# Running sums in PSUM for the first layer's Strassen products, and the last layer's weight sums moved from GpSimd to VectorE

## The chip, the core and the metric

The kernel runs on one core of one Trainium2 chip. The time is device microseconds; the lower, the better. The engines are named as in the profile: PE (TensorE matmul) with PEld (its weight loads), DVE (VectorE), ACT (ScalarE), POOL (GpSimd) and SP (SyncE, which issues most of the DMAs).

## The reference

Two layers run one after the other on `x` of 32 sequences x 128 tokens x 512 channels, all in float32.

```python
# layer 0: attention with 16 heads of 64, then experts chosen by the tokens' gates
shift = silu(t) @ W_ada.T + b_ada
h = _ln(x, ln1_g, ln1_b) + shift
qkv = (h @ Wqkv.T).reshape(b, n, 3, H, HD)
q = _ln(qkv[:, :, 0]...); k = _ln(qkv[:, :, 1]...); v = ...       # q and k are normalized per head
o = softmax(q k^T / sqrt(HD)) v
x = x + o @ Wout.T
tok = x.reshape(-1, d)
gate = softmax(tok @ Wgate.T)
vals, idx = top_k(gate.T, bs // E)          # E = 8 experts, each takes its best 512 of 4096 tokens
y = gelu(_ln(tok[idx]) @ fc1s[e].T + b1s) @ fc2s[e].T + b2s
tok = tok.at[idx].add(y * vals)
# layer 1: attention with 16 heads of 32, then an MLP of 2048, both behind an adaptive layer norm
normed = _layernorm(x) * (1 + scale) + shift
x = x + softmax(q k^T / sqrt(HD)) v @ wo.T + bo
x = x + gelu(normed @ w1.T + b1) @ w2.T + b2
```

## The kernel before

**Products.** Nearly all matmuls are done by Strassen's scheme in Winograd's form: a product of 2 x 2 blocks takes seven block products instead of eight, at the price of sums of blocks on both sides. With A and B cut into blocks and S and T for the block sums, the seven products are numbered 1: A11 B11, 2: A12 B21, 3: S4 B22, 4: A22 T4, 5: S1 T1, 6: S2 T2, 7: S3 T3. The four results are 1+2, 1+6+5+3, 1+6+7+4 and 1+6+7+5. In the last layer the MLP does this on two levels, 7 x 7, and needs sums of weights for it.

**First layer** (`pair`, some 60 to 940 us of the span). Sixteen pairs of sequences. From pair 1 on, the projections to q and k (two column groups, `q0` and `q1`) and to v are three calls of `seven` for each pair. A product there is two matmuls of 128 x 512 in float32, four matmul instructions. In the kernel before, each of the seven products has a PSUM bank of its own (`ps`, seven names; a bank is held from its product until it has been read). ScalarE copies product 1 to SBUF (`U1`, L1513) and VectorE makes seven additions (`comb`, L1509), each with one operand in PSUM: the running sums U2, U3, U4 in SBUF, and the four results. For q and k, ScalarE squares each result (`square`, L1471) and VectorE sums the squares per head (L1473). `back` does the attention of a sequence: transposes, scores, exponentials, sums, outputs. `project` is the output projection of a pair, again seven products (L1756, four matmuls of 128 x 256 each), with the residual `xt` added half by half: `onto` adds a running sum in SBUF, `out2` (L1772) a product in PSUM. For the last eight pairs (`LATE` is 16 sequences) the attention output is parked in DRAM and projected after all pairs (`late_projection`), while VectorE searches for the gates' thresholds.

**Experts** (`expert`, some 1060 to 1920 us). Eight experts. POOL makes the sums of the experts' weights, VectorE the additions to PSUM (`comb`, L2109, and `comb2`) and the masks `oh` of the next expert's tokens (L1926, 128 x 1024 in bf16); other block sums (`hs`, `tg`) go to either.

**Last layer** (from some 1920 us on). Here each set of seven products already uses three PSUM banks X, Y and Z: products 6, 7 and 4 are accumulated on top of product 1 in X, product 3 on top of product 5 in Z, and X and Z are read between (`chain_T`, L2571; `chained`, L2882; `seeded`, L2800). The sums of its MLP weights are made ahead and put in DRAM: 22 steps (`w1_outer`, `w2_outer`, `w1_inner`, `w2_inner`), each with four fetches of 256 KB, four sums (`weight_forms`) and four or seven stores. In the kernel before, four steps stand beside each of experts 0 to 4 and two beside expert 5, and POOL makes the sums. The like sums for wq, wk, wv and wo stand beside pairs 10 to 13, on VectorE.

**Order.** Every operation is given to a scheduler (`Sched`) with its engine or engines (`also`), an estimated duration, the buffers that it reads and writes, a priority and a job (pairs are jobs 0 to 15, then one for the routing, the experts, the last layer). The scheduler plays the program through with these estimates, admits jobs in a window of three, and on each engine takes what can start soonest, then what has the lowest priority number. The order found is the order of the program; each engine then runs its own list in order and waits on semaphores. `tt` is the helper for sums of two blocks in SBUF: VectorE (L1277) or POOL (L1278). It marks its operation with `port`: from job `lock_at` on, the plan lets no such operation of VectorE start while one of POOL runs, and the reverse. `lock_at` is the last layer's first job here. `keep` is the number of banks that must stay free when an operation takes one, `spare` the same for SBUF rows.

Of the kernel before, what the change touches and what calls it, by code (L numbers as in the profile page):

```python
# [186 lines left out]
class Op:  # L187
    __slots__ = ("alts", "prio", "job", "keep", "deps", "n", "ready", "next", "bufs", "lat", "done", "table", "seq", "mb", "port")


class Sched:
# [12 lines left out]
    def op(self, eng, us, fn, w=(), r=(), prio=0.0, job=0, keep=0, spare=0, lat=0.0, table=None, also=(), share=1.0, port=False):  # L204
# [5 lines left out]
        o.port = port  # L210
# [40 lines left out]
    def run(self):  # L251
# [46 lines left out]
        while left:  # L298
# [54 lines left out]
            for x in o.next:  # L353
                x.n -= 1
                wait = 0.0 if (len(x.alts) == 1 and e in x.alts and not lat) else self.WAIT[e]
                x.ready = max(x.ready, end + lat + wait)
# [804 lines left out]
def fast_kernel(ctx: ExitStack, tc: tile.TileContext, x, condT, mask, cols, w_ada, wqkv, wout, wout_p, wout_o, wgate,  # L1161
# [259 lines left out]
    def weight_sums():  # L1421
# [7 lines left out]
        for n in range(2):  # L1429
            for i, a_, b_, r_ in ((1, lambda n=n: wB(1, 2, n), lambda n=n: wB(1, 1, n), [wqkv_b[n + 2], wqkv_b[n]]),  # L1430
# [3 lines left out]
                tt(lambda i=i, n=n: wT(i, n), a_, b_, ALU.subtract, 2 * D, [wTb(i, n)], r_, 155, 1, DVE, False)  # L1434

    def pair(g):
# [48 lines left out]
        else:  # L1485
# [11 lines left out]
            def seven(name, B, T, pr, done):  # L1497

                ps = {m: bank(f"{name}{m}_{g}") for m in range(1, 8)}
                U1, U2, U3, U4 = (row(f"{name}u{m}_{g}") for m in "1234")  # L1500

                def prod(m, lhs, lb, rhs):
                    def f_():
                        for k in range(2):
                            nc.tensor.matmul(ps[m].t, lhs()[:, k, :], rhs[0](k), start=(k == 0), stop=(k == 1))  # L1505
                    sch.op(PE, mm_us(D, 2), f_, w=[ps[m]], r=[*lb, *rhs[1]], prio=pr, job=job, keep=3)

                def comb(o_, a_, m):
                    sch.op(DVE, dve_us(D), lambda: nc.vector.tensor_tensor(flat(o_), a_.t, ps[m].t, ALU.add), w=[o_],  # L1509
                           r=[a_, ps[m]], prio=pr, job=job)  # L1510

                prod(1, lambda: A(1, 1), rA(1, 1), B(1, 1))
                sch.op(ACT, act_us(D), lambda: nc.scalar.copy(U1.t, ps[1].t), w=[U1], r=[ps[1]], prio=pr - 1, job=job)  # L1513
                prod(2, lambda: A(1, 2), rA(1, 2), B(2, 1))
                done(comb, 1, 1, U1, 2)
                prod(6, lambda: Sv(2), [Sb[2]], T(2))
                comb(U2, U1, 6)
                prod(7, lambda: Sv(3), [Sb[3]], T(3))
                comb(U3, U2, 7)
                prod(5, lambda: Sv(1), [Sb[1]], T(1))  # L1520
# [878 lines left out]
    for n, step in enumerate(steps):  # L2399
        e = n // 4  # L2400
        step(5000.0 + 1000 * e + 800, RJ + 1 + e)
# [658 lines left out]
```

## Time and profile before

| | |
|---|---|
| median of 3 runs | 3227.43 us (3227.32 to 3228.43) |
| the profiled execution's own time | 3228.02 us |
| its span in the profile | 3226.3 us |
| mean granted clock of PE | 0.99 |
| PE busy | 3122.8 us (97%) |
| DVE busy | 2389.7 us (74%) |
| ACT busy | 1171.3 us (36%) |
| POOL busy | 1124.2 us (35%) |
| DMA | 460.02 MB, mean 143 GB/s |

Busy time is the sum of the time in which an engine has an instruction under way[...]. A line such as `L1277` is the line of the kernel that issued the instruction; since helpers issue many of them, the names of the tiles tell which they are. A wait is put down to the operation that came last before the waiting one went on. Queries of the trace by stretches of time show which engine limits a stage; the totals above mix stages with different limits.

### The profile page before, as it was taken

The numbers are of one execution on the slowest core, as the hardware profiler recorded it, in microseconds if no ns is written. First come the engines' busy times: TensorE is split into PE (matmuls) and PEld (weight loads), VectorE is DVE, ScalarE is ACT, GpSimd is POOL, SyncE is SP. The second block draws the span as 40 slices with busy tenths as digits, with TensorE's granted clock in tenths as the row PEclk, the third lists the DMA queues.
The fourth block names the chain that finished last, engine by engine and source line by source line (L and its number), as shares of the span: only waits on it lengthen the run. The fifth ranks groups of instructions, "written<-read, shape, count | busy, mean of one in ns | idle before, by whom it ended". The sixth has DMA issues, their size and how long they took to land. (4 is left out here: it accounts for less than half of the span.)

```text
span 3226.3 us, 60396 instructions
## 1 busy us (share of the span) xinstructions
PE 3122.8 (97%) x22740; PEld 2539.3 (79%) x22740; DVE 2389.7 (74%) x4834; ACT 1171.3 (36%) x2962; POOL 1124.2 (35%) x858
## 2 busy tenths in 40 slices
PE   9999999999999999989899999999999999999988
PEld 5655665555568888778788888989899999898988
DVE  8877767888778886876776536776868686868685
ACT  4333333434430212221122214545454545353533
POOL 0111110000030477767766520333333333333335
PEclk9999999999999999999999999999999999999999
DMA  4111112232245564676445261655655565555557
GB/s 174 47 57 46 44 44 69 89 99 64 64 146 174 158 185 155 189 211 187 160 156 158 79 193 35 202 185 166 188 161 187 161 190 165 183 175 173 181 178 228
DMA packets 293455, 460.02 MB, mean 143 GB/s; under 512 B 29930, under 2 KB 111394, under 8 KB 293154
## 3 DMA queue, kind: packets, MB, share of 16 engines
q1 hardware_dynamic: 284498, 438.43, 42.7%
q0 software_dynamic: 7168, 16.91, 2.7%
q8 instruction: 183, 3.00, 0.4%
q14 instruction: 118, 0.97, 0.1%
q10 hardware_dynamic: 1488, 0.71, 0.1%
HBM read 383.44 MB, written 72.51 MB: 141 GB/s over the span
## 5 line engine op out<-in xcount | busy, mean ns | idle before, releaser
L1278 POOL TENSOR_TENSOR base<-base,base 128x512 f32<-128x512 f32 x330 | 437.5, 1337 | 854.4 <-DVE base L2851 278.1
L2882 PE MATMUL bank<-base,base 128*128 128x128 f32 x3080 | 369.0, 277 | 14.0 <-DVE base L2727 7.7
L2800 PE MATMUL bank<-base,base 128*128 128x128 f32 x3080 | 376.3, 277 | 6.0 <-DVE base L1277 3.1
L2800 PEld LDWEIGHTS bank<-base,base 128*128 128x128 f32 x3080 | 366.5, 193 | 12.6 <-ACT bank L2761 3.5
L2882 PEld LDWEIGHTS bank<-base,base 128*128 128x128 f32 x3080 | 355.0, 192 | 24.9 <-DVE base L2727 9.5
L1277 DVE TENSOR_TENSOR base<-base,base 128x512 f32<-128x512 f32 (+2 forms) x487 | 298.4, 636 | 18.7 <-PE bank L2882 3.6
L2115 ACT ACTIVATE h<-h,prm 128x256 f32<-128x256 f32 x256 | 115.2, 500 | 324.0 <-DVE h L2109 314.7
L2168 PE MATMUL d<-fc,h 128*128 128x256 f32 x992 | 221.8, 383 | 0.6 <-PE pi L1946 0.4
L2168 PEld LDWEIGHTS d<-fc,h 128*128 128x128 f32 x992 | 189.6, 192 | 27.4 <-ACT h L2115 0.6
L2104 PE MATMUL u<-gT,fc 128*128 128x256 f32 x768 | 182.8, 389 | 23.5 <-DVE h L2109 22.8
L2810 ACT ACTIVATE base<-base,prm 128x128 f32<-128x128 f32 x512 | 169.9, 395 | 48.1 <-DVE base L2845 28.3
L2104 PEld LDWEIGHTS u<-gT,fc 128*128 128x128 f32 x768 | 149.8, 196 | 46.5 <-DVE h L2109 24.0
L1471 ACT ACTIVATE sq<-qk 128x512 f32<-128x512 f32 x128 | 81.3, 635 | 283.0 <-DVE qk L1509 271.1
L2104 PE MATMUL u<-tg,s 128*128 128x256 f32 x512 | 124.9, 388 | 13.0 <-DVE h L2109 8.0
L2104 PEld LDWEIGHTS u<-tg,s 128*128 128x128 f32 x512 | 98.9, 194 | 29.0 <-issue 8.6
L2109 DVE TENSOR_TENSOR h<-v,u 128x512 f32<-128x512 f32 x128 | 86.2, 681 | 45.9 <-PE u L2104 44.6
L2845 DVE TENSOR_TENSOR base<-bank,base 128x512 f32<-128x512 f32 x96 | 66.0, 687 | 72.1 <-PE bank L2800 56.8
L2168 PE MATMUL d<-t,hs 128*128 128x256 f32 x512 | 113.4, 379 | 0.0
L1505 PE MATMUL q<-wqkv,hsb 128*128 128x512 f32 x240 | 113.4, 595 | 0.0
L1505 PE MATMUL q<-t,hsa 128*128 128x512 f32 x240 | 112.8, 592 | 0.0
L1505 PE MATMUL q<-wqkv,hT 128*128 128x512 f32 x240 | 111.5, 598 | 0.0
L2727 DVE TENSOR_TENSOR base<-bank,base 128x128 f32<-128x128 f32 x168 | 47.7, 288 | 82.5 <-PE bank L2882 67.7
(1154 smaller groups left out, 6703.7 us busy)
## 6 DMA issues: line engine op xcount, KB each, us to landing
base<-w1i SPq DMA_DIRECT2D x224, 256.0 KB, 3.3
base<-w2i SPq DMA_DIRECT2D x224, 256.0 KB, 3.5
base<-w2s SPq DMA_DIRECT2D x168, 256.0 KB, 3.0
fc<-in_fc_dram SPq DMA_DIRECT2D x64, 512.0 KB, 7.6
fc<-in_fc_dram SPq DMA_DIRECT2D x32, 1024.0 KB, 8.5
base<-w1s SPq DMA_DIRECT2D x96, 256.0 KB, 3.4
base<-in_w_dram SPq DMA_DIRECT2D x72, 256.0 KB, 3.7
x<-in_x_dram SPq DMA_DIRECT2D x32, 256.0 KB, 3.7
```

Of the source, the lines that this page charges most:

```text
L1277: ways = {DVE: (DVE, dve_us(n), lambda: nc.vector.tensor_tensor(o_(), a_(), b_(), op_)), POOL: (POOL, 0.2 + n / 480, lambda: nc.gpsimd.ten ...
L1278: POOL: (POOL, 0.2 + n / 480, lambda: nc.gpsimd.tensor_tensor(o_(), a_(), b_(), op_))}
L1471: sch.op(ACT, act_us(D), lambda: nc.scalar.activation(sq.t, qk[i][j].t, AF.Square), w=[sq], r=[qk[i][j]], prio=pr, job=job)
L1505: nc.tensor.matmul(ps[m].t, lhs()[:, k, :], rhs[0](k), start=(k == 0), stop=(k == 1))
L2104: nc.tensor.matmul(ps[n].t[:, t, :], lhs()[:, k, t * P : (t + 1) * P], rhs.t[:, k, :], start=(k == 0), stop=(k == 1))
L2109: sch.op(DVE, dve_us(D), lambda: nc.vector.tensor_tensor(o_.t, a_.t, ps[n].t, ALU.add), w=[o_], r=[a_, ps[n]], prio=pr, job=job)
L2115: sch.op(ACT, act_us(HQ, 1), lambda t=t, c=c: nc.scalar.activation(o_.t[:, t, :], o_.t[:, t, :], AF.Gelu_apprx_tanh, bias=col("b1s", e * 1 ...
L2168: nc.tensor.matmul(ps[n].t[:, j, :], lhs[m].t[:, k, t * P : (t + 1) * P], rhs.t[:, 2 * m + k, :], start=(m == 0 and k == 0), stop=(m == NM ...
L2800: nc.tensor.matmul(b_.t[:, u, :], w_.t[:, u * P : (u + 1) * P], x_(), start=fresh and u == 0, stop=True, skip_group_check=True)
L2810: sch.op(ACT, act_us(S, 1), lambda k=k, u=u, c=c: nc.scalar.activation(o_[k].t[:, u * S : (u + 1) * S], o_[k].t[:, u * S : (u + 1) * S], A ...
L2845: sch.op(DVE, dve_us(D), lambda: nc.vector.tensor_tensor(d_[k].t, flat(src), first[k].t, ALU.add), w=[d_[k]], r=[src, first[k]], prio=po - ...
L2882: nc.tensor.matmul(b_.t, x_()[:, k * S : (k + 1) * S], w_.t[:, k, :], start=fresh and k == 0, stop=True, skip_group_check=True)
```

## The change

In `seven` and in `project`, the seven products use three banks X, Y, Z, in the order 1 (X), 5 (Z), 2 (Y), 6 (onto X), 3 (onto Z), 7 (onto X), 4 (onto X); in `seven` products 3 and 7 stand in this order, and product 4 last. Between the accumulations X and Z are read. In `seven` the readings are four copies (`kept`: u1, t_, u2 and one result; ScalarE or VectorE, whichever the plan finds free) and three VectorE additions. In `project` they are seven additions to the residual by VectorE, and `onto` and the copy are gone.

The sums of `weight_forms` go from POOL to VectorE, and the 22 steps from experts 0 to 5 to pairs 3 to 13, two steps beside each pair. Their fetches no longer wait for an expert (`ups`). Their stores get `late`, by which the plan has their readers wait 8 us longer. The sums t12 and t4 of the q and k weights may run on POOL too. `lock_at` is 0: the plan takes the port into account from the start.

```diff
-    def op(self, eng, us, fn, w=(), r=(), prio=0.0, job=0, keep=0, spare=0, lat=0.0, table=None, also=(), share=1.0, port=False):
+    def op(self, eng, us, fn, w=(), r=(), prio=0.0, job=0, keep=0, spare=0, lat=0.0, table=None, also=(), share=1.0, port=False, late=0.0):
...
-                x.ready = max(x.ready, end + lat + wait)
+                x.ready = max(x.ready, end + lat + wait + x.late)
...
-                tt(lambda i=i, n=n: wT(i, n), a_, b_, ALU.subtract, 2 * D, [wTb(i, n)], r_, 155, 1, DVE, False)
+                tt(lambda i=i, n=n: wT(i, n), a_, b_, ALU.subtract, 2 * D, [wTb(i, n)], r_, 155, 1)
...
-            def seven(name, B, T, pr, done):
-                ps = {m: bank(f"{name}{m}_{g}") for m in range(1, 8)}
-                U1, U2, U3, U4 = (row(f"{name}u{m}_{g}") for m in "1234")
-                def prod(m, lhs, lb, rhs):
-                    def f_():
-                        for k in range(2):
-                            nc.tensor.matmul(ps[m].t, lhs()[:, k, :], rhs[0](k), start=(k == 0), stop=(k == 1))
-                    sch.op(PE, mm_us(D, 2), f_, w=[ps[m]], r=[*lb, *rhs[1]], prio=pr, job=job, keep=3)
-                prod(1, lambda: A(1, 1), rA(1, 1), B(1, 1))
-                sch.op(ACT, act_us(D), lambda: nc.scalar.copy(U1.t, ps[1].t), w=[U1], r=[ps[1]], prio=pr - 1, job=job)
-                prod(2, lambda: A(1, 2), rA(1, 2), B(2, 1))
-                done(comb, 1, 1, U1, 2)
-                prod(6, lambda: Sv(2), [Sb[2]], T(2))
-                comb(U2, U1, 6)
-                prod(7, lambda: Sv(3), [Sb[3]], T(3))
-                comb(U3, U2, 7)
-                prod(5, lambda: Sv(1), [Sb[1]], T(1))
-                done(comb, 2, 2, U3, 5)
-                comb(U4, U2, 5)
-                prod(4, lambda: A(2, 2), rA(2, 2), T(4))
-                done(comb, 2, 1, U3, 4)
-                prod(3, lambda: Sv(4), [Sb[4]], B(2, 2))
-                done(comb, 1, 2, U4, 3)
+            def seven(name, B, T, pr, dest, done):
+                X, Y, Z = (bank(f"{name}{c}_{g}") for c in "xyz")
+                u1, u2, t_ = (row(f"{name}{c}_{g}") for c in "rst")
+                def prod(b_, lhs, lb, rhs, fresh, also=(), keep=0):
+                    def f_():
+                        for k in range(2):
+                            nc.tensor.matmul(b_.t, lhs()[:, k, :], rhs[0](k), start=fresh and k == 0, stop=True, skip_group_check=True)
+                    sch.op(PE, mm_us(D, 2), f_, w=[b_], r=[*lb, *rhs[1], *also], prio=pr, job=job, keep=keep)
+                def comb(i, l, a_, b_):
+                    o_ = dest(i, l)
+                    sch.op(DVE, dve_us(D), lambda: nc.vector.tensor_tensor(flat(o_), a_.t, b_.t, ALU.add), w=[o_], r=[a_, b_], prio=pr, job=job)
+                    done(i, l)
+                def kept(o_, src):
+                    copy([o_], [src], lambda: flat(o_), lambda: src.t, D, pr - 60, job)
+                prod(X, lambda: A(1, 1), rA(1, 1), B(1, 1), True, [Y, Z], 2)
+                prod(Z, lambda: Sv(1), [Sb[1]], T(1), True)
+                kept(u1, X)
+                prod(Y, lambda: A(1, 2), rA(1, 2), B(2, 1), True)
+                kept(t_, Z)
+                prod(X, lambda: Sv(2), [Sb[2]], T(2), False)
+                comb(1, 1, Y, u1)
+                kept(u2, X)
+                prod(Z, lambda: Sv(4), [Sb[4]], B(2, 2), False)
+                prod(X, lambda: Sv(3), [Sb[3]], T(3), False)
+                comb(1, 2, Z, u2)
+                comb(2, 2, X, t_)
+                prod(X, lambda: A(2, 2), rA(2, 2), T(4), False)
+                kept(dest(2, 1), X)
+                done(2, 1)
...
+        X, Y, Z = (bank(f"w{c}_{g}", (P, HD)) for c in "xyz")
+        def out2(i, l, b_):
+            sch.op(DVE, dve_us(HD), lambda: nc.vector.tensor_tensor(half(i, l), b_.t, half(i, l), ALU.add),
+                   w=[(xt[i - 1], l)], r=[b_, (xt[i - 1], l)], prio=pr - 60, job=job)
+        prod(X, A(1, 1), *B(1, 1), True, [Y, Z], 1)
+        prod(Z, S_[1], *T(1), True)
+        out2(1, 1, X)
+        prod(Y, A(1, 2), *B(2, 1), True)
+        out2(2, 2, Z)
+        prod(X, S_[2], *T(2), False)
+        out2(1, 1, Y)
+        out2(1, 2, X)
+        prod(Z, S_[4], *B(2, 2), False)
+        prod(X, S_[3], *T(3), False)
+        out2(1, 2, Z)
+        send(1)
+        out2(2, 2, X)
+        prod(X, A(2, 2), *T(4), False)
+        out2(2, 1, X)
+        send(2)
...
-        sch.op(SP, 0.06, lambda: nc.sync.dma_start(b_.t, src), w=[b_], r=[*r, ups[job - RJ - 1]], lat=4.0, prio=pr, job=job, spare=12)
+        sch.op(SP, 0.06, lambda: nc.sync.dma_start(b_.t, src), w=[b_], r=r, lat=4.0, prio=pr, job=job, spare=12)
...
-        sch.op(SP, 0.06, lambda: nc.sync.dma_start(dst, flat(b_)), w=[(std, key)], r=[b_], lat=4.0, prio=pr, job=job)
+        sch.op(SP, 0.06, lambda: nc.sync.dma_start(dst, flat(b_)), w=[(std, key)], r=[b_], lat=4.0, prio=pr, job=job, late=8.0)
...
-            tt(lambda o_=o_: o_.t, lambda a_=a_: a_.t, lambda b_=b_: b_.t, op_, D, [o_], [a_, b_], pr, job, POOL, False)
+            tt(lambda o_=o_: o_.t, lambda a_=a_: a_.t, lambda b_=b_: b_.t, op_, D, [o_], [a_, b_], pr, job, DVE, False)
...
-        e = n // 4
-        step(5000.0 + 1000 * e + 800, RJ + 1 + e)
+        g = 3 + n // 2
+        step(200.0 * g + 190, g)
...
-    st.sch.lock_at = LJ
+    st.sch.lock_at = 0
```

## The prediction

> **What bounds the kernel now.** I read the busy time by stage first, cut at the kernel's own boundaries (200 to 900 us is first layer; each expert is one cut, experts 1 to 7 start at 1170, 1276, 1385, 1499, 1611, 1720, 1820; the last layer follows). Shown are the first layer, expert 3 and expert 6. Columns: length, busy us of PE, PEld, DVE, ACT, POOL, granted clock, DMA share, GB/s.
>
> ```profile
> 200.00:900.00 700.00, 699.91 (x4937) 410.57 (x4928) 535.72 (x1238) 271.34 (x706) 60.22 (x54) 1.00 0.21 65
> ...
> 1385.00:1499.00 114.00, 101.77 (x498) 89.14 (x497) 86.45 (x103) 23.15 (x52) 82.52 (x64) 0.94 0.58 173
> ...
> 1720.00:1820.00 100.00, 98.97 (x466) 86.78 (x465) 64.40 (x77) 22.44 (x50) 58.33 (x42) 1.00 0.37 98
> ```
>
> Two things are to be seen. In the first layer PE is never idle, so nothing there can be gained by relieving VectorE (77% busy) or ScalarE (39%); new waits there, however, add to the time one for one. And experts 1 to 5, the same work as expert 6, take 106, 109, 114, 112 and 109 us where expert 6 takes 100: 550 against 500, so 50 us are lost, part as PE idle and part as a lower clock. Expert 6 has no weight sums for the last layer; POOL is busy 58 us there, 76 to 84 in the others.
>
> Next the waits of PE, asked for 1400 to 1500, 1500 to 1600, 1600 to 1700 and 1700 to 1900 us (one answer line each), then PE, VectorE and POOL in order of time around the first of them:
>
> ```profile
> PE u L2104 <- DVE h L2109: 12.2, 1, 12.2
> PE u L2104 <- DVE h L2109: 10.0, 1, 10.0
> PE u L2104 <- DVE h L2109: 6.3, 1, 6.3
> PE u L2104 <- DVE h L2109: 1.0, 1, 1.0
> ```
>
> ```profile
> 1409.07 3.62 PE L2104 MATMUL u<-gT,fc 128*128 128x256 f32 x16
> 1433.56 5.91 PE L2104 MATMUL u<-gT,fc 128*128 128x256 f32 x16 [12.23 <-DVE h L2109]
> ```
>
> ```profile
> 1413.70 19.20 DVE L1926 TENSOR_TENSOR oh<-iota_jb,lo 128x1024 bf16<-128x1024 bf16 x1
> 1432.83 0.67 DVE L2109 TENSOR_TENSOR h<-v,u 128x512 f32<-128x512 f32 x1
> ```
>
> ```profile
> 1415.42 1.83 POOL L1278 TENSOR_TENSOR w1n_4f<-w1r,w1n_4f 128x512 f32<-128x512 f32 x1
> 1416.65 5.46 POOL L1278 TENSOR_TENSOR t<-fc,fc 128x512 f32<-128x512 f32 x4
> 1421.54 5.42 POOL L1278 TENSOR_TENSOR t<-fc,t 128x512 f32<-128x512 f32 x4
> 1426.42 5.39 POOL L1278 TENSOR_TENSOR fc<-fc,fc 128x512 f32<-128x512 f32 x4
> ```
>
> A VectorE operation with two SBUF inputs (`oh`, 1.22 us when free) stands for 19.20 us, until POOL's unbroken run of 15 sums ends at 1431.8. The PSUM addition queued behind it (L2109) then frees a bank for PE, which has idled 12.23 us and afterwards runs 16 matmuls in 5.91 us instead of 3.62: the half clock. The first three of the 15, from 1412.96 on, are sums for the last layer (`w1n_4f` and its like). Expert 6 shows the same thing without them:
>
> ```profile
> 1745.96 13.40 DVE L1277 TENSOR_TENSOR hs<-h,h 128x512 f32<-128x512 f32 x1 [0.97 <-ACT h L2115]
> ```
>
> ```profile
> 1760.83 1.97 PE L2104 MATMUL u<-tg,s 128*128 128x256 f32 x8 [1.03 <-DVE h L2109]
> ```
>
> A block of 13.40 us costs PE 1.03 us: PE's work ahead covers 12.4 us there, 7.0 at 1413 (19.20 less 12.23).
>
> **The change part by part.**
>
> *Weight sums to VectorE and to pairs 3 to 13 (two steps a pair).* The 22 steps have 4 sums each, 88 in all. They leave POOL, where sums in a run start 1.23 us apart: 108 us go, 16 sums or 20 us per expert in 0 to 4 and 8 sums in expert 5. On VectorE the nearest rows are the sums for wq, wk, wv and wo, which already run there in pairs 10 to 13:
>
> ```profile
> L1277 DVE TENSOR_TENSOR os__6712<-os__6701,oq 128x512 f32<-128x512 f32 x1 | 0.7, 694 | 0.0
> ```
>
> 88 x 0.69 = 61 us. Their DMAs move too: 88 fetches and 100 stores of 256 KB (4 and 4 a step, 7 stores in the four `w2_outer`), 48 MB. Pairs 3 to 13 take some 640 us (their first L1505 matmuls start at 195 and, for pair 14, at 838), so 75 GB/s join the 65 of the first row; 140 is less than the experts carry now. On SP's queue a store waits for its sum, and behind it wait loads of x, xT and the statistics; the sums of wq to wo with their stores already stand so in pairs 10 to 13, and PE has no wait there. I cost this at nothing; the cover is that loads land 3 to 4 us after issue and are early: from 200 to 900 us the normalization (L1600) waits 0.5 us in all for a transfer. If the cover fails, each late load stops PE for a few us.
>
> *What this gives in the experts.* [...] The trace says that a VectorE operation stands until a whole run of POOL operations is over (19.20 us for 15). [...] By the row the gain is the 50 us. The measurement decides. What remains is POOL's run of 12 (`t`, `t`, `fc`: 1416.65 to 1431.8, 15 us), a block of up to 15 us; against a cover of 7 to 12 PE would wait 3 to 8 us, against expert 6's example 1 us. Bounds of the gain: 15 us (8 us and the colder clock in most experts) to 51. I take expert 6's 1 us in each of five: 50 - 4 = 46 us.
>
> *Planner's lock from the start, `late` of 8 us for stores, t12 sums also on POOL.* Only the order changes. The lock makes the plan know that `hs` cannot pass a POOL run, but `oh` isn't marked, so it can still be caught. Worth -5 to +5 us; I take 0, as nothing in the trace tells the sign.
>
> *The sevens on running sums.* 45 of them (three in each of 15 pairs). PE's work stays: 7 products of 4 matmul instructions. In PE's order of time, groups of eight instructions of 256 columns start 1.73 us apart, so four of 512 take 1.73. VectorE's PSUM additions fall from 7 to 3, copies rise from 1 to 4:
>
> ```profile
> L1509 DVE TENSOR_TENSOR qk<-q0u,q 128x512 f32<-128x512 f32 x49 | 33.5, 683 | 25.7 <-PE q L1505 25.5
> L1513 ACT COPY q0u<-q 128x512 f32<-128x512 f32 x12 | 7.0, 587 | 17.7 <-PE q L1505 16.2 <-DVE xn L1600 1.5
> ```
>
> VectorE: -180 x 0.683 = -123 us, with the sums +61, so 62 us less over the 870 us of these pairs: 77% becomes about 70%. ScalarE: +135 x 0.587 = 79 us: 39% becomes 48%. Neither is the bound; this work lies beside PE. What lies on the path is new: before, each product had its own bank; now X is added to by products 6, 7 and 4 only after X was read. Between 1 and 6 stand two products, 3.5 us, for a copy of 0.59 us; between 6 and 7 one, 1.73 us; between 7 and 4 none of its own, so an addition of 0.68 us and two semaphores must be covered by another seven or by attention. Behind PE's waiting matmul everything of PE is queued. Three banks of eight are held for a whole seven.
>
> The trace of before has this scheme already, in the last layer:
>
> ```profile
>   DVE base L1277: 0.4, 1
>   issue: 0.2, 1
> ```
>
> ```profile
>   DVE base L2727: 17.2, 18
>   issue: 13.1, 30
> ```
>
> These are the idle lists of PE (us, times) by what ended the idle time: first of L2571, 32 chains of the last layer's projections, 0.6 us in all; then of L2882, 56 chains of its MLP, 36 us with the smaller entries. Per chain 0.02 to 0.64 us. Products there last half as long as here, so the cover was smaller. With 45 sevens and 16 projections, 61 chains: 1 to 39 us. I take 10, since L2571, two chains beside attention as here, is the nearer row.
>
> [...] If it came to the 0.94 of expert 3, 870 us would grow by 6%, 52 us, and the change would lose. But the last layer, made of such chains, has a granted clock of 1.00 here:
>
> ```profile
> 2400.00:2500.00 100.00, 96.81 (x968) 90.07 (x968) 82.14 (x179) 48.58 (x125) 35.19 (x27) 1.00 0.63 196
> ```
>
> So I add nothing for it.
>
> *Projections.* 16; PE's 7 products stay. From 3 + 4 PSUM additions, 4 SBUF additions and a copy to 7 PSUM additions of 0.42 us: 4 x 0.42 x 16 = 27 us less on VectorE and POOL, off the path. Their waits are in the 61 chains.
>
> *Sum.* The profiled execution took 3228.0 us (span 3226.3 and 1.7 around it), the median is 3227.4. 3228.0 - 46 + 10 = 3192.0; less 0.6 for the median, 3191 us.
>
> **The rivals.** (1) *POOL's own run of 12 is enough*: experts keep waits of 3 to 8 us, which cool the clock too, and half is recovered, 25 us: 3227 - 25 + 10 = 3212. For it: `oh` isn't marked. Against it: expert 6, which has the run and waits 1 us. (2) *The chains cost as L2882's do*, 36 to 39 us with the experts' 46: 3219. For it: VectorE at 70% and ScalarE at 48% now sit in PE's path. (3) *Slower: PE waits at X.* An addition or copy queued late behind ScalarE's squares (which waited 223.6 us for VectorE from 200 to 900) or VectorE's sums stops PE at products 7 and 4. It decides from 46 / 61 = 0.75 us per chain; at 1.0 us it is 61 us: 3242. Against it: 1.0 is above both rows. (4) *The planner's order is no better anywhere, or the moved sums hold up pairs*: gain and loss within a few us of each other, 3227.
>
> **How the numbers follow.** My forecast 0.55 (own range 3178 to 3203), rival 1 0.17, rival 2 0.13, rival 3 0.09, rival 4 0.06. Predicted 3191. The low end takes a full 51 us with chains at 1 us, 3177; the high end reaches into rivals 1 and 2, 3222. A measurement tells 0.2% (6.5 us) from no change. Faster 0.85, same 0.06, slower 0.09.
>
> **What would show it.** Right: experts 1 to 5 near 100 us each at clock 1.00, no VectorE operation above 15 us there, POOL near 58 us an expert; first-layer PE idle of some 10 us, put down to L1509's or a copy's successors. Wrong: blocks of 13 to 15 us with PE waits above 3 us (rival 1), PE waits for copies or additions in nearly every seven (rivals 2 and 3), PE waiting for transfers of x or xT between 300 and 850 us (SP's queue).

## The result, and the profile after

The changed kernel takes 3202.45 us (median of four runs, 3200.34 to 3203.46), beside 3227.93 for the kernel before in the same comparison: a ratio of 0.9917, 95% interval 0.9900 to 0.9934, so 25 us faster. Its profiled execution took 3203.46 us with a span of 3201.7.

Where did the 25 us come from? I cut both profiled spans at the same four points: the first L1505 matmul (pair 1's first product), the last L1505 matmul (the end of pair 15's products), the first matmul of expert 0 (L2104 before, L2090 after), and the first chained product of the last layer (L2571 before, L2557 after). Lengths in us:

| | before | after | difference |
|---|---|---|---|
| up to pair 1's first product | 66.7 | 87.4 | +20.7 |
| pairs 1 to 15, first to last L1505 matmul | 872.0 | 879.2 | +7.2 |
| late projections and hand-over to the experts | 129.7 | 130.2 | +0.5 |
| the eight experts | 863.3 | 810.1 | -53.2 |
| last layer | 1294.6 | 1294.8 | +0.2 |
| span | 3226.3 | 3201.7 | -24.6 |

So two large numbers stand against each other: the experts gave 53 us, more than forecast, and the front took 28 back. By these cuts most of it lies ahead of pair 1's first product, where the forecast put nothing; but the new order also moves that product within the work, so the split of the 28 us is settled by the experiments only.

The busy time by stage of the changed kernel, for the same stages as before: the first layer, expert 3, expert 6 (lines have moved, and expert 3 now runs from 1399 to 1498, expert 6 from 1697 to 1795). Columns: length, busy us of PE, PEld, DVE, ACT, POOL, granted clock, DMA share, GB/s.

```profile
200.00:900.00 700.00, 698.58 (x4843) 401.41 (x4842) 493.86 (x1162) 326.45 (x774) 55.42 (x42) 1.00 0.37 124
1399.00:1498.00 99.00, 99.00 (x496) 87.42 (x495) 66.49 (x104) 21.84 (x48) 65.84 (x48) 1.00 0.39 110
1697.00:1795.00 98.00, 98.00 (x463) 86.43 (x462) 56.99 (x71) 21.76 (x48) 55.86 (x41) 1.00 0.35 97
```

Read the expert rows first: PE is busy for the whole of 99 us at clock 1.00, where it was busy 101.77 of 114 us at clock 0.94. From 1200 to 1795 us, experts 1 to 6, the waits of PE list nothing at all. In the first layer PE is still full, VectorE is down to 493.86 of 700 us (71%), ScalarE up to 326.45 (47%), and the traffic has nearly doubled from 65 to 124 GB/s.

VectorE in the changed expert 3, and POOL beside it, in order of time:

```profile
1411.37 0.68 DVE L2095 TENSOR_TENSOR h<-v,u 128x512 f32<-128x512 f32 x1
1411.97 10.41 DVE L1912 TENSOR_TENSOR oh<-iota_jb,lo 128x1024 bf16<-128x1024 bf16 x2
```

```profile
1410.56 2.33 POOL L2186 DMA_INDIRECT acc<-y,idx  x1 [3.92 <-DVE h L2095]
1412.34 5.50 POOL L1278 TENSOR_TENSOR t<-fc,fc 128x512 f32<-128x512 f32 x4
1417.24 1.81 POOL L1278 TENSOR_TENSOR hs<-h,h 128x512 f32<-128x512 f32 x1
1419.13 2.17 POOL L1278 TENSOR_TENSOR hs<-hs,h 128x512 f32<-128x512 f32 x1
```

The block has not gone: the first `oh` of the two takes 8.2 us, where 19.2 were seen before. But POOL's run is now short, 8.2 us lies inside the work that PE has ahead, and PE does not notice.

Now the part that was not expected. The two largest of PE's waits from 57 to 160 us in the changed kernel (us in total, times, longest), and the stretch from 60 to 85 us by engine:

```profile
PE sc L1658 <- DVE qkT L1638: 10.8, 1, 10.8
PE tpx L1250 <- DVE xn L1591: 1.2, 1, 1.2
```

```profile
60.00:85.00 25.00, 12.95 (x106) 11.39 (x108) 21.14 (x42) 7.65 (x23) 10.79 (x5) 0.66 0.00 1
```

VectorE, then POOL, then PE in order of time at that place:

```profile
59.27 2.28 DVE L431 TENSOR_SCALAR qk_1y<-var 128x32 int32<-128x32 int32 x1
61.58 2.27 DVE L435 SCALAR_TENSOR_TENSOR qk_1t<-qk_1y 128x32 f32<-128x32 f32 x1
63.89 0.19 DVE L437 TENSOR_TENSOR qk_1t<-qk_1t,var 128x32 f32<-128x32 f32 x1
64.11 2.22 DVE L439 SCALAR_TENSOR_TENSOR qk_1y<-qk_1t,qk_1y 128x32 f32<-128x32 f32 x1
```

```profile
59.15 2.36 POOL L1278 TENSOR_TENSOR t<-wqkv,t 128x1024 f32<-128x1024 f32 x1
61.46 2.35 POOL L1278 TENSOR_TENSOR t<-wqkv,wqkv 128x1024 f32<-128x1024 f32 x1
63.88 2.40 POOL L1278 TENSOR_TENSOR t<-wqkv,t 128x1024 f32<-128x1024 f32 x1
```

```profile
72.15 3.79 PE L1658 MATMUL sc<-qkT,qkT 64*128 64x128 f32 x32 [10.77 <-DVE qkT L1638]
87.44 1.88 PE L1505 MATMUL q0x<-wqkv,hT 128*128 128x512 f32 x4
```

The t12 sums (`t<-wqkv`) now also run on POOL, each 2.3 us long. Beside them VectorE makes a short, serial series of operations on 32 columns, 0.19 us each when free, and five of them take 2.2 to 2.3 us and end only when POOL's sum of the moment ends. 10.77 us of PE idle follow, and then the 32 `sc` matmuls take 3.79 us, with PE busy for all of it at a granted clock of 0.50 (2.06 us in e1 below, which does not have this wait).

### The profile page after: what moved, and what is told of

It is laid out like the page before. It is cut to its first block, busy times and chain, and to the rows that moved or that the text cites. A ratio compares the mean times of both kernels' runs of the same rounds, so it can differ in the third digit from the quotient of the medians.

```text
span 3201.7 us, 60112 instructions
## 1 busy us (share of the span) xinstructions
PE 3127.3 (98%) x22740; PEld 2536.5 (79%) x22740; DVE 2231.2 (70%) x4706; ACT 1238.5 (39%) x3048; POOL 1036.6 (32%) x775
## 5 line engine op out<-in xcount | busy, mean ns | idle before, releaser
L2090 PE MATMUL u<-gT,fc 128*128 128x256 f32 x768 | 178.9, 383 | 0.5 <-ACT gT L2053 0.5
L2090 PEld LDWEIGHTS u<-gT,fc 128*128 128x128 f32 x768 | 147.5, 192 | 21.4 <-ACT gT L2053 0.9
L1473 DVE TENSOR_REDUCE var<-sq 128x8 f32<-128x512 f32 x128 | 86.7, 678 | 62.1 <-ACT sq L1471 61.5
L2090 PE MATMUL u<-tg,s 128*128 128x256 f32 x512 | 121.0, 379 | 0.3 <-DVE tg L1277 0.3
L2090 PEld LDWEIGHTS u<-tg,s 128*128 128x128 f32 x512 | 97.2, 190 | 13.9 <-issue 0.7
L2154 PEld LDWEIGHTS d<-t,hs 128*128 128x128 f32 x512 | 97.2, 190 | 13.2
L2617 ACT ACTIVATE base<-bank,mbT 128x512 f32<-128x512 f32 x128 | 82.1, 688 | 51.3 <-PE bank L2613 42.5
```

Of the source, the lines that this page charges most:

```text
L1473: sch.op(DVE, dve_us(D), lambda: nc.vector.tensor_reduce(var[i].t[:, j * 8 : (j + 1) * 8], sq.t, AX.X, ALU.add), w=[(var[i], j)], r=[sq], ...
L2090: nc.tensor.matmul(ps[n].t[:, t, :], lhs()[:, k, t * P : (t + 1) * P], rhs.t[:, k, :], start=(k == 0), stop=(k == 1))
L2154: nc.tensor.matmul(ps[n].t[:, j, :], lhs[m].t[:, k, t * P : (t + 1) * P], rhs.t[:, 2 * m + k, :], start=(m == 0 and k == 0), stop=(m == NM ...
L2617: sch.op(ACT, act_us(D, 1), lambda sc=scs[r], pe=pe[r], b=b: nc.scalar.activation(pe.t, sc.t, AF.Exp, bias=mbT[:, b : b + 1], scale=sm1), ...
```

## The experiments

The theory after the result had four parts. (1) The experts' gain is the weight sums leaving POOL and the experts. (2) The front loses through the t12 sums on POOL. (3) It also loses through the running sums, but at pair 1, not through waits at X spread over all pairs. (4) VectorE had room for the weight sums without the running sums. The rivals were that the planner's lock did it, that the running sums were needed to make room, and that the chains wait everywhere. Each ratio below is against the kernel before on the same chip. That kernel took 3225.6 to 3230.8 us on the chips used, so kernels of different comparisons are best set side by side by their ratios or by the stages of their profiles. How far a stage can be trusted: e2 and e10 below change nothing ahead of the experts but, in e2, the order, and start expert 0 at 1067.5 and 1069.3 us, within 1 us of the kernel before (1068.4). *Port*, in the code and in the expectations, stands for no more than the time for which an operation of VectorE or of POOL is held up beside the other's; no trace shows what lies behind it.

**e1: the changed kernel with the t12 sums on VectorE, as before.**

```
-                tt(... ALU.subtract, 2 * D, [wTb(i, n)], r_, 155, 1)
+                tt(... ALU.subtract, 2 * D, [wTb(i, n)], r_, 155, 1, DVE, False)
```

> The changed kernel with one line undone: the t12 and t4 sums of the q and k weights stay on VectorE alone. In the changed kernel POOL makes them in one run from 59 to 71 us, and VectorE's Newton steps for the second sequence (128x32, 0.19 us when free) take 2.2 to 2.3 us each beside it; PE then waits 11.0 us at 61 us and runs on half clock. Theory: this placement alone is the 20.7 us that the start loses (first product of pair 1 at 87.4 us against 66.7). Then the first product of pair 1 is at 66 to 72 us, and the kernel takes 3182 to 3190. Rival: the start is lost to the new order of pair 0 (the lock in the plan, the chains' banks), and the line does nothing: 3200 to 3204.

3196.1 us, ratio 0.9911 (0.9894 to 0.9927). The first product is back at 67.9 us (66.7 before), but expert 0 starts at 1090.9, only 5.9 us earlier than the changed kernel's 1096.8. The time lies between the theory and the rival, and neither holds: the placement of the t12 sums is worth 5.9 us, not 20.7. From pair 1's first product to pair 2's it is now 82.8 us (64.2 before, 68.4 in the changed kernel); how much of this is a real loss is taken up at e6. PE's waits from 57 to 155 us come to 8.3 us (2.8 before, from 57 to 135), and its granted clock from 60 to 155 us is 0.96 (1.00 before). The three largest waits:

```profile
PE q0z L1505 <- DVE hsa L1277: 2.7, 1, 2.7
PE tpx L1250 <- DVE xn L1591: 2.4, 2, 1.6
PE wx L1755 <- issue: 2.2, 1, 2.2
```

PE of e1, then of the kernel before, at that place in order of time:

```profile
67.89 1.98 PE L1505 MATMUL q0x<-wqkv,hT 128*128 128x512 f32 x4
71.67 1.98 PE L1505 MATMUL q0y<-wqkv,hT 128*128 128x512 f32 x4
...
90.95 3.35 PE L1505 MATMUL q0z<-t,hsa 128*128 128x512 f32 x4 [2.75 <-DVE hsa L1277]
```

```profile
66.66 1.98 PE L1505 MATMUL q<-wqkv,hT 128*128 128x512 f32 x4
72.41 5.42 PE L1505 MATMUL q<-wqkv,hT 128*128 128x512 f32 x12
85.05 3.60 PE L1505 MATMUL v<-wqkv,hT 128*128 128x512 f32 x8
```

In the kernel before, six products that need no weight or sequence sums (`q`, `v` from `wqkv` and `hT`: 4, 12 and 8 matmuls) fill the time in which VectorE makes those sums. With running sums only two come so early, `q0x` and `q0y`; then PE waits for `hsa`, a sum of VectorE's. That the three banks held for a seven keep the rest out is what the code says; the trace shows only that they come late.

**e2: the kernel before with the planner's lock from the start.**

```
-    st.sch.lock_at = LJ
+    st.sch.lock_at = 0
```

> The kernel before with lock_at = 0 and nothing else: only the planned order changes, the sums for the last layer stay on POOL beside the experts. Theory (the experts were slow because POOL's load of sums made long unbroken runs): the runs stay, experts 1 to 5 still take 106 to 114 us, and the gain is under 15 us: 3213 to 3235. Rival (the plan was at fault, since it didn't know of the port): experts 1 to 5 fall to about 100 us each, a gain of 35 to 50 us: 3177 to 3193.

3208.35 us, ratio 0.9945 (0.9928 to 0.9961). Expert 0 starts at 1067.5 (1068.4), the experts take 846.4 us (863.3). So the plan alone is worth 17 us in the experts while the weight sums are there, a little more than the theory allowed and far less than the rival's 35 to 50; blocks of VectorE of 21.5 and 19.8 us remain.

**e3: the kernel before with the weight sums moved to pairs 3 to 13, on VectorE; no running sums, no lock.** The stores' `late` of 8 us and the loads without their old condition belong to it.

```
-            tt(lambda o_=o_: o_.t, ... D, [o_], [a_, b_], pr, job, POOL, False)
+            tt(lambda o_=o_: o_.t, ... D, [o_], [a_, b_], pr, job, DVE, False)
...
-        e = n // 4
-        step(5000.0 + 1000 * e + 800, RJ + 1 + e)
+        g = 3 + n // 2
+        step(200.0 * g + 190, g)
```

> The kernel before with the 22 steps of weight sums moved to pairs 3 to 13 and to VectorE, with their late stores, and nothing else: seven banks a seven, lock_at as before. Theory: the experts gain 45 to 53 us by the move alone. VectorE in pairs 8 to 13 is 80 to 84% busy and gets 5.5 us more per 52 us, about 94%, so PE may wait there: 0 to 20 us given back; 3175 to 3198. Rival (plan at fault): oh and hs are still caught behind POOL's run of 12, the experts gain less than 25 us: 3203 to 3225. Second rival (the running sums were needed to make room on VectorE): the pairs lose 30 us or more: 3205 to 3225.

3179.64 us, ratio 0.9857 (0.9841 to 0.9874). The experts take 811.3 us, as in the changed kernel (810.1), and pairs 1 to 15 take 874.8 (872.0). The theory holds and both rivals fall: the running sums are not needed to make room, and without them the gain is 46 us instead of 25.

**e4: the kernel before with the running sums only** (`seven` and `project` of the change, whole).

```
-                ps = {m: bank(f"{name}{m}_{g}") for m in range(1, 8)}
+                X, Y, Z = (bank(f"{name}{c}_{g}") for c in "xyz")
...
-        ps = {n: bank(f"w{n}_{g}", (P, HD)) for n in range(1, 8)}
+        X, Y, Z = (bank(f"w{c}_{g}", (P, HD)) for c in "xyz")
```

> The kernel before with the running sums in PSUM for seven and project, and nothing else. Theory: pairs 1 to 15 take about 7 us more than before (879 against 872 us, as in the changed kernel), the experts still lose 50 us: 3232 to 3240. Rival: VectorE's relief (120 us less of additions) speeds up the pairs or the late projections: 3215 to 3226. Second rival: the chains alone lose more than in the changed kernel, since POOL's and VectorE's order there was made with the lock: above 3245.

3236.93 us, ratio 1.0036 (1.0024 to 1.0047): slower by 11 us, as the theory had it. Expert 0 starts 11.2 us later, experts and last layer stay (862.8 and 1292.7). From pair 1's first product to pair 2's it is 81.7 us, much as in e1. From 200 to 900 us PE's waits list nothing: the loss is not one of long waits at X.

**e5: e3 with the lock from the start.**

```
-    st.sch.lock_at = LJ
+    st.sch.lock_at = 0
```

> The kernel before with the weight sums moved to pairs 3 to 13 and VectorE (as in the run that moved them alone, 3179.6) and lock_at = 0 besides; no running sums, t12 on VectorE. Theory: the lock gained 17 us in experts 1 to 5 only because POOL's runs with the last layer's sums were there; with these gone the experts are at 99.3 us each and nothing is left to gain: 3176 to 3184. Rival: the two gains add up, 3160 to 3168.

3175.93 us, ratio 0.9829 (0.9813 to 0.9845). Expert 0 starts at 1072.6 (1073.0 in e3), the experts take 809.5 (811.3). The two gains do not add up to the rival's 3160 to 3168. This is the fastest kernel measured here: it is the change without its running sums and with the t12 sums on VectorE.

**e6: e1 with the old sevens of seven banks in pair 1 only.**

```
+            if g == 1:
+                seven = seven_old
```

> The changed kernel with t12 on VectorE (3196.1) and the three sevens of pair 1 as before, a bank for each product; the sevens of pairs 2 to 15 and all projections stay on running sums. Theory: the running sums lose at one place, pair 1. There the second sequence and the weight sums come late, and before PE went ahead with products 1 and 2 of q0, q1 and v, six products or 10.3 us that need neither; three banks held by the first seven leave no bank to begin the next, so PE goes idle and cools down. Then the time from pair 1's first product to pair 2's falls from 82.8 to 65 to 70 us: 3179 to 3188. Rival: the loss is the order of the products (5 stands second and needs sums of weights and of the second sequence) or the projections' waits, and seven banks alone don't mend it: 3192 to 3197.

3192.47 us, ratio 0.9882 (0.9866 to 0.9899). The time lies where the rival put it, although pair 2's first product is at 134.0 us instead of 150.7, as the theory said. That gain of 16.7 us is mostly not real. Where the form changes, the first product of the next pair moves to another place in PE's order, so its start is no fair mark between a pair with seven banks and one with three: the next stretch, from pair 2's first product to pair 3's, is 75.5 us (65.2 in e1), and still e6 loses nothing to e1 in it. The marks that have the same form in both kernels say so: the first product of pair 2's projection (`wx`) is at 204.6 us, 6.4 earlier than in e1 (211.0), pair 3's first product 6.4 earlier (209.4 and 215.8), pair 15's 6.3 earlier (907.5 and 913.7), and expert 0 starts 5.4 earlier (1085.5). PE of e6, then of e1:

```profile
204.55 1.99 PE L1792 MATMUL wx<-wout,oT 128*128 128x256 f32 x8
209.40 1.88 PE L1505 MATMUL q0x<-wqkv,hT 128*128 128x512 f32 x4
```

```profile
210.96 1.99 PE L1755 MATMUL wx<-wout,oT 128*128 128x256 f32 x8
215.81 1.88 PE L1505 MATMUL q0x<-wqkv,hT 128*128 128x512 f32 x4
```

So pair 1 accounts for about 6 us of what the running sums cost, and that much stays repaired. Since e6 gives pair 1 its old order of products as well as its banks, it does not tell which of the two matters.

**e7: e3 with the weight sums moved to the pairs but left on POOL.**

```
-        e = n // 4
-        step(5000.0 + 1000 * e + 800, RJ + 1 + e)
+        g = 3 + n // 2
+        step(200.0 * g + 190, g)
```

> The kernel before with the weight sums moved to pairs 3 to 13 but made by POOL as before: place changed, engine not. Theory: what counts for the experts is that POOL's sums are not there; POOL has some 90% idle beside the pairs, so experts at 99.3 to 100 us each, and the pairs lose a little where VectorE's sums and POOL's runs of four (5 us) meet: 3174 to 3190. Rival: beside the pairs POOL's runs block VectorE as they did in the experts, and PE, which has no slack there, waits: above 3195.

3211.35 us, ratio 0.9943 (0.9927 to 0.996). The experts gain just the same (811.4 us), but pairs 1 to 15 take 905.4 us instead of 874.8, so the rival holds: beside the pairs POOL's sums make PE wait. PE is idle for 19.8 of the 605 us from 300 to 905 us; the largest entries of its waits:

```profile
PE tpq L1250 <- DVE qk L1509: 5.1, 5, 2.6
PE sc L1658 <- DVE qkT L1638: 3.1, 3, 1.3
PE tpq L1250 <- DVE qk L1626: 2.4, 2, 2.2
```

**e10: the kernel before with the weight sums on VectorE, left beside the experts.**

```
-            tt(lambda o_=o_: o_.t, ... D, [o_], [a_, b_], pr, job, POOL, False)
+            tt(lambda o_=o_: o_.t, ... D, [o_], [a_, b_], pr, job, DVE, False)
```

> The kernel before with the 88 weight sums on VectorE but left where they were, beside the experts. With e7 (the pairs, POOL) this makes a square of place and engine. Theory (in the experts it is POOL's runs that hold VectorE; the place does not matter once POOL no longer makes the sums): experts fall to about 815 to 825 us, start of the experts unchanged at 1068, last layer 1294, in all 3178 to 3190. Rival (VectorE, already busy 75 to 85 us of each of these experts, cannot take 11 us more there without PE waiting for h and u): experts stay at 835 to 860, in all 3200 to 3225.

3204.8 us, ratio 0.9915 (0.9898 to 0.9932). The rival is right and my theory here is wrong: experts of 841.3 us, not 815 to 825. Only one block above 6 us is left (14.6 us), yet PE waits some 23 us in all from 1066 to 1907 us, most of it for VectorE's `h` and `v`:

```profile
PE tpg L1250 <- DVE h L2109: 5.9, 2, 5.6
PE u L2104 <- DVE v L2109: 5.5, 5, 3.4
PE tpg L1250 <- DVE v L2109: 4.0, 3, 2.7
PE d L2168 <- PE pi L1946: 2.0, 5, 0.5
PE u L2104 <- DVE h L2109: 1.8, 1, 1.8
```

With before, e3 and e7 this is a square. Length in us of pairs 1 to 15, and of the experts:

| weight sums | on POOL | on VectorE |
|---|---|---|
| beside the experts | 872.0, 863.3 (before) | 872.0, 841.3 (e10) |
| beside pairs 3 to 13 | 905.4, 811.4 (e7) | 874.8, 811.3 (e3) |

In the experts the engine is worth 22 us and the place another 30; in the pairs the engine is worth 31. Both halves of the move were needed for the whole gain.

**e11: the changed kernel with the lock only from the last layer on.**

```
-    st.sch.lock_at = 0
+    st.sch.lock_at = LJ
```

> The kernel after with the planner's lock switched on only at the last layer, as before; all else as after. Theory (the lock is worth nothing in the pairs once POOL's sums are few, the t12 sums and the chains make the loss in front): start of the experts within 3 us of after's 1096.8, experts within 3 us of 810, in all 3199 to 3206. Rival (the lock, not only POOL's t12 sums, is what reorders the front of the kernel, and carries the part of its 28 us that the parts run singly do not add up to): start of the experts 1085 to 1092, in all 3190 to 3197.

3202.49 us, ratio 0.9909 (0.9893 to 0.9926); expert 0 starts at 1096.0, the experts take 811.5. The theory holds: once the weight sums are gone from POOL, the lock is worth nothing.

**e12: e1 with the old sevens in all pairs, so that only the projections keep running sums.**

```
+            seven = seven_old
```

> The kernel after with the t12 sums on VectorE and the sevens of every pair as in the kernel before (seven banks, seven additions); only the projections keep their running sums in three banks. Against e5 it shows the 16 projections' running sums alone. Theory (the sevens carry what the running sums cost in front of the experts, since they hold up pair 1 and are 45 of 61 chains): start of the experts 1072 to 1077, pair 2's first product at about 133, experts 810, in all 3175 to 3182. Rival (the projections carry it, because three held banks of a projection keep the next pair's first products out): start of the experts 1083 to 1090, in all 3187 to 3195.

3183.16 us, ratio 0.9864 (0.9848 to 0.9881). Expert 0 starts at 1077.7: just outside the theory's range (as is the time) and far from the rival's. The sevens carry the larger share, but the projections are not free.

Taken from e5 one edit at a time, the start of expert 0 moves as follows: before 1068.4; weight sums and lock 1072.6 (+4.2, e5); running sums in the projections 1077.7 (+5.1, e12); in the sevens 1090.9 (+13.2, e1); t12 sums on POOL 1096.8 (+5.9, after). The order matters: running sums alone cost 11.2 us on the kernel before (e4), 18.3 on e5. The difference lies in the pairs behind the first. From the first product of each pair to that of the next, pairs 2 to 7 and 9 to 14 together (pair 8, where the projections stop, moves the mark) take, in us:

| | seven banks | running sums |
|---|---|---|
| weight sums beside the experts | 694.6 (before) | 695.2 (e4) |
| weight sums beside the pairs, on VectorE | 695.6 (e3), 692.5 (e5) | 702.7 (e1), 702.8 (after) |

Each part alone costs these twelve pairs 1 us or less; the two together cost 8, some 0.7 us a pair.

**e8 and e9: VectorE's operations beside POOL's sums, by themselves.** The whole argument of the forecast hung on how long POOL holds VectorE out, so I measured it in two small kernels that hold nothing of the model. In e8 POOL makes 12 sums (or 6 wide ones), independent or each from the one before; VectorE makes reductions and then one kind of operation (code shortened).

```
for k in range(1, 12):
    nc.gpsimd.tensor_tensor(g[k], a, b, ALU.add)      # chained: g[k - 1] in place of a
...
nc.vector.tensor_tensor(dc, a, b, ALU.add)            # or small, from PSUM, with one input
```

> No part of the computation: it measures the port alone. 16 cases one after the other; in each POOL makes a run of 12 sums of 128x512 (or 7, six of them 128x1024), independent of each other or each reading the one before, and VectorE does three reductions (one SBUF input), then the operation under test, a reduction again. Tested: one sum of two SBUF blocks 128x512; four scalar_tensor_tensor of 128x32; three sums with one operand in PSUM; one tensor_scalar of 128x512. The reading from the kernels: beside a run of independent sums the two-input operation stands until the run is over (10 us or more of 14.7), beside chained ones it gets in after one sum (at most 1.3 us, or 2.4 for 128x1024, as at 59 to 71 us of the changed kernel); the PSUM sums and reductions take what they take alone, 0.68 us. [...]

VectorE's operations in e8, in order of time: a sum beside 12 independent sums; three with an operand in PSUM (`psx`) beside the same; a sum beside 12 chained sums; a sum beside wide chained sums:

```profile
9.94 1.03 DVE L76 TENSOR_TENSOR dc<-a,b 128x512 f32<-128x512 f32 x1
41.37 2.13 DVE L79 TENSOR_TENSOR dp<-psx,b 128x512 f32<-128x512 f32 x3
72.53 1.15 DVE L76 TENSOR_TENSOR dc<-a,b 128x512 f32<-128x512 f32 x1
204.35 2.11 DVE L76 TENSOR_TENSOR dc<-a,b 128x512 f32<-128x512 f32 x1
```

A sum that takes 0.69 us free takes at most 1.15 in e8 beside sums of 1.26 us and 2.11 beside wide ones: the 0.3 to 1.4 us more are no longer than one POOL sum (1.26 us here, 2.3 us for a wide one in the changed kernel), far from the run. The three with an operand in PSUM were not held up (2.13 us, 0.71 each); an operation with one SBUF input took 0.77 to 0.89 us beside the narrow sums and 1.85 beside the wide ones. Four operations of 128x32, the kind of the chain at 59 us above, took 8.50 us beside wide independent sums, some 2.1 each. This contradicts both the expectation and what I had read from the 19.20 us. But in the traces of the kernel before and of the changed one each VectorE operation of over 6.3 us (19.20, 19.73, 17.70 and 13.40 us before; four of 8.2 and one of 6.40 after) began beside a run of POOL sums that an indirect DMA leads, and so did e10's block of 14.6: `DMA_INDIRECT` at 1410.56 us in the changed kernel, and in the kernel before

```profile
1411.93 1.56 POOL L2200 DMA_INDIRECT acc<-y,idx  x1 [4.42 <-DMA acc<-y,idx]
```

So in e9 an indirect DMA is set ahead of the sums (code shortened).

```
+            scatter() or gather()   # indirect DMA, 128 rows of 512
             for k in range(1, 12):
                 nc.gpsimd.tensor_tensor(g[k], a, b, ALU.add)
```

> A small kernel that computes only this: seven times over, POOL does 12 independent 128x512 sums in SBUF while VectorE does reductions and then two 128x512 sums in SBUF some microseconds later. Between POOL's first sum and the other eleven stands nothing, or an indirect scatter-add into DRAM, or an indirect gather from DRAM; in one case the scatter is followed by two sums and then a sum that waits for VectorE, in one a second scatter stands in the middle. It leaves out the whole model. Theory (the indirect DMA changes how POOL's following sums hold the port): without it VectorE's sum takes at most 2.3 us and POOL's rows show 1.26 us each; after a scatter or gather POOL's rows show 1.8 us each and VectorE's sum stands until the run ends, 8 us or more; behind the sum that waited it is 2.3 us again. Rival (the indirect DMA is a bystander, and what makes the whole run block is something else of the experts, such as transfers to the same memory): at most 2.3 us in every case.

POOL of e9, then VectorE: nothing between (from 6.28 us), a scatter (22.67), a gather (43.65), a scatter and then a sum that waits (64.01):

```profile
6.28 1.26 POOL L45 TENSOR_TENSOR g<-dv,b 128x512 f32<-128x512 f32 x1 [0.81 <-DVE dv L65]
7.50 14.37 POOL L45 TENSOR_TENSOR g<-a,b 128x512 f32<-128x512 f32 x11
...
24.10 1.66 POOL L48 DMA_INDIRECT acc<-b,idx  x1 [0.17 <-issue]
25.25 13.94 POOL L45 TENSOR_TENSOR g<-a,b 128x512 f32<-128x512 f32 x11
...
45.06 1.01 POOL L52 DMA_INDIRECT xg<-acc,idx  x1
46.10 13.44 POOL L45 TENSOR_TENSOR g<-a,b 128x512 f32<-128x512 f32 x11
...
72.60 1.26 POOL L45 TENSOR_TENSOR g<-ds,b 128x512 f32<-128x512 f32 x1 [3.07 <-DVE ds L74]
73.82 10.70 POOL L45 TENSOR_TENSOR g<-a,b 128x512 f32<-128x512 f32 x8
```

```profile
11.17 1.81 DVE L84 TENSOR_TENSOR dc<-a,b 128x512 f32<-128x512 f32 x1
...
27.55 12.19 DVE L84 TENSOR_TENSOR dc<-a,b 128x512 f32<-128x512 f32 x1
...
48.54 11.56 DVE L84 TENSOR_TENSOR dc<-a,b 128x512 f32<-128x512 f32 x1
...
74.41 1.22 DVE L84 TENSOR_TENSOR dc<-a,b 128x512 f32<-128x512 f32 x1
```

The same 11 sums hold the same VectorE sum for 1.81 us without an indirect DMA ahead and for 12.19 or 11.56 us, to the end of the run, with one; a repeat gave 1.81 and 12.07. Where one of POOL's sums waits for VectorE, a VectorE sum behind that takes 1.22 us, 9 us after the scatter; without the wait the block was still standing 15 us after it, so the passing of these 15 us did not end it. Where a second scatter stands between five sums and six more, VectorE's sum got in there after 4.79 us, and the next one was held for 7.37. The theory holds and the rival, that the indirect DMA is a bystander, falls. One part of the theory does not hold: POOL's rows of 1.8 us stand behind the scatters only; behind the gather they show 1.25 to 1.27 us, and VectorE is held all the same. Why POOL behaves so, the profile does not show.

## Why the prediction was right, and where its steps were not

The time of 3202.45 lies at the upper end of the forecast's own range of 3178 to 3203, and that is partly luck: the cost in front of the experts was 28 us where 10 were forecast, and 7 us more of gain than forecast made up for some of it. Of the four terms three were off.

*"550 against 500, so 50 us are lost"; gain 46 us.* That the weight sums made the loss is shown by e3: moving them alone takes the experts from 863.3 to 811.3. The size was 53.2. Experts 1 to 5 now take 99.3 us each and not 100.8. Expert 6 was not a clean template: it had a block of 13.40 us and a wait of 1.03 itself, and shrank to 98.4; and the run of 12 POOL sums that was to stay beside the others came out as runs of six.

*"A VectorE operation stands until a whole run of POOL operations is over".* The row was the right one for the experts, but not because every run of POOL sums holds VectorE: it was taken for a rule of all runs, and in e8 a sum was held for no longer than one of POOL's (1.03 to 1.15 us beside narrow sums, 2.11 beside wide ones, for 0.69). In e9 the row holds behind an indirect DMA with no wait after it (12.19 and 11.56 us). Rival 1 (POOL's run of 12 is enough) did not come about in the changed kernel, where the longest blocks were 8.2 us; a block of that kind did in e10, 14.6 us.

*Weight sums beside the first layer: "I cost this at nothing".* Nearly so by themselves: e3 starts the experts 4.6 us later than before and e5 4.2; they lose it in different places, and I leave its cause open. Together with the running sums they cost 7 us more (the table behind e12). The named cover, early loads, held at 124 GB/s: no entry of PE's waits between 200 and 900 us is a transfer.

*Planner's lock and t12: 0, "-5 to +5".* The lock is 0 (e11), though in the kernel before it would have been 17 us (e2). The t12 sums cost 5.9 us, above the bound. The step that failed is that it was bounded as a matter of order: 128x1024 sums on POOL stood beside a serial chain of small VectorE operations that PE waits for, and five of those paid the rest of a POOL sum (2.2 to 2.3 us for 0.19).

*Running sums: "chains +10 us", as waits at X.* The size for the step alone came out near (11.2 in e4), but not by the mechanism that gave it. Nobody waits at X for long: from 200 to 900 us PE's listed waits in the changed kernel are 1.0 us in all, none of them for a copy or for L1510. What the forecast passed over is at pair 1, where the products that ran ahead come late; its own half sentence "Three banks of eight are held for a whole seven" names the likely reason, which no run separates from the new order of the products. With the weight sums beside it, as in the change, the step costs 18.3 us: about 6 at pair 1 (e6) and some 10 spread thinly over pairs 2 to 7 and 9 to 14 (702.7 us against e5's 692.5); the rest is not placed. The spread part has next to no listed wait behind it. At less than 1 us a pair, which has three or four chains, it may hold waits at X too short for the list, which would be the forecast's own mechanism; that is not settled.

*The granted clock in the pairs: "I add nothing for it".* The forecast weighed a fall to expert 3's 0.94; the granted clock is 1.00 from 200 to 900 us. From 57 to 900 us of the changed kernel it is below 1.00 only in the wait of 10.77 us at 61 us and behind it: 0.50 from 72.15 to 80 us, 0.88 from 80 to 85, 1.00 from 85 to 900. In the 5.91 us of the kernel before that the forecast put down to the half clock it is 0.62 (0.50 in the first 2.44 us).

*VectorE to 70%, ScalarE to 48%.* Measured 71% and 47%, and worth nothing, as said.

*Rivals 2 and 3.* Listed waits in nearly every seven did not come. But a change with only this part would have ended on rival 3's side, slower (e4), mainly by another mechanism.

Sum: forecast -46 + 10 + 0 + 0 = -36; measured, in the profiles' stages, -53.2 for the experts, +18.3 for running sums, +5.9 for t12, +4.2 for the weight sums and lock, +0.2 for the last layer, -24.6.

## What to carry to other kernels

A product form that holds fewer banks, each for longer and in a new order, can take away work that ran ahead; look for its price at the first iteration, where the other inputs are still late (about 6 us here), and then beside other new work, where it can cost a little in every iteration (some 0.7 us a pair here) though neither alone costs more than 1 us over twelve pairs. Sums moved to POOL can be paid for again on VectorE (5.9 us for the t12 sums, 31 for the weight sums beside the pairs): keep them away from short serial chains of VectorE that PE waits for, and keep a run of them behind an indirect DMA shorter than the work that PE has ahead (8.2 us cost nothing here, 19.2 us cost 12). When the order of a program changes, the start of a stage's first operation can move without any time being won or lost; compare where both kernels have the same form. When a change has several parts, try each alone: here the fastest kernel (3175.9 us) is the change with one part and one line left out.

## What the runs showed that I had not expected

With an indirect DMA ahead of them, POOL's sums held up VectorE's for the whole run (e9): a sum of VectorE took 12.19 us (scatter) or 11.56 us (gather) instead of 1.81 us beside the same 11 POOL sums, and 1.22 us once one of POOL's sums had waited. Behind the scatters such a run is marked by POOL rows that overlap (1.83 us each at a spacing of 1.23 in the kernel before, where other sums show 1.27 us); behind e9's gather the rows do not show it (1.25 to 1.27 us).
